# Three seams of an eight-sublayer network on one core: a stage's last group finished inside the next stage, ends beside batches, norms on ScalarE

## The chip, the cores and the metric

The kernel is one program on one core of a Trainium2 chip. It holds five engines with a queue each: TensorE (PE, with its weight loads listed as PEld), VectorE (DVE), ScalarE (ACT), GpSimd (POOL) and SyncE (SP), which issues all the DMAs of this kernel. Each engine works through its own queue in order. The metric is the device time of one execution in microseconds. The time before is the median of three runs.

## The reference

The network has four layers, each of an attention-like and a feed-forward sublayer, over 16 sequences of 256 tokens with 128 features:

```python
x = L0_attn_inputs                                   # (16, 256, 128), float32
x = x + _layernorm(_L0_attn_ref(_layernorm(x), ...)) # attention with masked scores
x = x + _layernorm(_L0_ffn_ref(_layernorm(x), ...))  # gated, weights from int32
x = x + _layernorm(_L1_attn_ref(_layernorm(x), ...)) # 4 blocks: mixed attention + MLP
x = x + _layernorm(_L1_ffn_ref(_layernorm(x), ...))  # soft mixture of 64 experts
x = x + _layernorm(_L2_attn_ref(_layernorm(x), ...)) # 16-head causal attention
x = x + _layernorm(_L2_ffn_ref(_layernorm(x), ...))
x = x + _layernorm(_L3_attn_ref(_layernorm(x), ...)) # scan, MLP, attention, MLP
x = x + _layernorm(_L3_ffn_ref(_layernorm(x), ...))  # experts chosen by top-k

def _layernorm(x, axis=-1, eps=1e-05):
    m = jnp.mean(x, axis=axis, keepdims=True)
    v = jnp.var(x, axis=axis, keepdims=True)
    return (x - m) / jnp.sqrt(v + eps)
```

Within `_L1_attn_ref` each of the four depths first normalises x again with a gain and a bias (`ln1_g`, `ln1_b`) and adds its attention, then does the same with `ln2_g`, `ln2_b` and an MLP with gelu. The mixture of `_L1_ffn_ref` is the part with two softmaxes:

```python
logits = jnp.einsum('bmd,dnp->bmnp', x, phi)
dispatch = jax.nn.softmax(logits, axis=0)            # over the 16 sequences
combine = jax.nn.softmax(logits.reshape(bsz, m, n * p), axis=-1).reshape(bsz, m, n, p)
slots = jnp.einsum('bmd,bmnp->bnpd', x, dispatch)
y = jnp.einsum('bnpd,nde->bnpe', slots, W) + b[None, :, None, :]
out = jnp.einsum('bnpd,bmnp->bmd', y, combine)
```

## The kernel before

The tokens lie in SBUF as eight groups, x[0] to x[7]. A group is two sequences: 128 partitions by NT = 4 tiles of 128 tokens by D = 128 features. z[0] to z[7] hold the input of a sublayer in the same form. The program is a row of stages: stage_l0 (layer 0, both sublayers), stage_l1_attn, stage_soft_moe (the mixture), stage_l2_attn and so on. Each stage opens a pool of work tiles in SBUF and one in PSUM, and closes them when it has emitted its last instruction. The next stage's tiles lie in the same memory, so its first instructions on those tiles wait until the last instructions of the closed pools have ended. The names of PSUM tiles in the profile are those of the rings (ps_s, ps_o, ps_mm, ps_t), whichever computation uses them.

A layer norm is made of these pieces. `stats` (L243 to L257 in the profile) gives four BATCH_NORM_STATS2 (ln_st) and four aggregates (ln_mv) on VectorE, then `rsqrt` on GpSimd: a TENSOR_SCALAR (L244) and a power (L245), both of 128x4, which give rs. `normed` (L264) subtracts the mean and multiplies by rs in four TENSOR_SCALAR on VectorE. In stage_l0 there is another form of its own, which makes nb = -mean * rs on GpSimd (L577, L578) and then normalises with four ACTIVATE on ScalarE (L583). `residual` normalises y into ln_y and adds it to x on GpSimd (L284).

The pieces of work of one group are Python generators. What follows a `yield` is emitted later, after what the other active generators emit. stage_l0 gives its order by hand (`turns`, a group every four steps). stage_l1_attn uses `interleave` with five active generators: the 8 `l1_mix` and then the 8 `ffn` generators of each of the four depths. `l1_norm_T` at the head of each makes a norm, four transposes against the identity (L306) and a copy with gain and bias on ScalarE (L776), and gives hT (xT in the profile) to the projections wq, wk and tok. In `l1_mix` VectorE reduces the first part of tok (qm, q; L831, L832) and the maxima of the scores (l_max, L854), then adds them into q2T (L868); the second scores give e (ScalarE, L901), masked on GpSimd (L904), and oT (L917). In the last depth `ffn` goes on with the residual to x[g] and with `then(g)`, which is `fill`: it stores x[g] to DRAM as xs and makes mxn[g], the norm that the mixture reads. Outside the stages ordered by hand a scheduler places the instructions of the generators on the engines' queues; the final order on each queue is fixed when the program is built.

stage_l1_attn begins with its constants: six memsets of l1_val and l1_lin, four of l1_max and l1_ctx, two copies into l1_ctx, all on GpSimd (L746 to L750), and two casts on VectorE (L753).

The mixture works through eight blocks of experts. In turn n it runs `share(n)`, `logits(n + 2)` and `slots(n + 1)` side by side. `share` takes the 16 sequences b in turn: exponentials, four transposes, a copy (meT), the product with y (ps_o), and two updates of x per b on VectorE (L1145), with the sums copied by ScalarE (mgot, L1148). In the last turn, when only `share` is left, the two sequences of a group are followed by `end(g)`:

```python
back = k.t([P, NT, D], "slT", 3)
nc.sync.dma_start(out=back, in_=xs[:, g])
...
v.tensor_tensor(xg, xg, bc(r.rearrange("p t b -> p b t"), 3, D), ALU.mult)
n = yield from k.norm(x[g], "mdisp", 3)
nc.gpsimd.tensor_tensor(x[g], back, n, ALU.add)
```

Here r (mend in the profile, L1164 to L1166) is one over the sum of weights, L1168 is the multiplication, mdisp the normalised result and L1170 the addition on GpSimd. stage_l2_attn then begins with `head(0)`, whose norm (xn) comes from x[0], and with `attention_pools`, memsets of at_vm and at_pc on GpSimd (L344 to L349) and casts on VectorE (L356). The keys are spread over heads as km (two ACTIVATE, one GpSimd product L364), and only then does the first score matmul run.

Of the kernel before, what the change touches and what calls it, by code (L numbers as in the profile page):

```python
# [185 lines left out]
def idle(n):  # L186

    for _ in range(n):
        yield


def bc(ap, axis, n):

    ap = ap.unsqueeze(axis)
    shape = list(ap.shape)
    shape[axis] = n
    return ap.to_broadcast(shape)


class Ctx:  # L200
# [61 lines left out]
    def normed(self, out, src, mv, rs):  # L262
        for k in range(NT):
            self.nc.vector.tensor_scalar(  # L264
                out[:, k, :], src[:, k, :], mv[:, k, 0:1], rs[:, k : k + 1], ALU.subtract, ALU.mult
            )
# [277 lines left out]
def stage_l0(k, x, w, wv, wi, z):  # L544
# [27 lines left out]

    def stats(src):

        mv, rs = k.stats(src)
        nb = k.t([P, NT], "ln_nb", 6)
        gp.tensor_scalar(nb, mv[:, :, 0], -1.0, None, ALU.mult)  # L577
        gp.tensor_tensor(nb, nb, rs, ALU.mult)  # L578
        return nb, rs

    def normed(out, src, nb, rs):
        for t in range(NT):
            nc.scalar.activation(  # L583
                out[:, t, :], src[:, t, :], AF.Identity, bias=nb[:, t : t + 1], scale=rs[:, t : t + 1]
            )
# [62 lines left out]
    def group(g):  # L648
        nb, rs = stats(x[g])
        yield from idle(2)  # L650
        xn = k.t([P, NT, D], "xn", 2)
        normed(xn, x[g], nb, rs)
# [38 lines left out]
        nb, rs = stats(x[g])  # L691
        yield from idle(2)
        xn = k.t([P, NT, D], "xf", 2)
        normed(xn, x[g], nb, rs)
# [23 lines left out]
        y = k.t([P, NT, D], "y", 3)  # L718
        nc.scalar.copy(y, ps)
        yield  # L720
        mv, rs = k.stats(y)
# [4 lines left out]
        nb, rs = stats(x[g])  # L726
        yield from idle(2)
        normed(z[g], x[g], nb, rs)
        yield

# [4 lines left out]
def stage_l1_attn(k, x, ws, rows, z, then):  # L735
# [9 lines left out]
    for a in k.l1_val + k.l1_lin:  # L745
        nc.gpsimd.memset(a, 1.0)  # L746
# [17 lines left out]
    for i in range(4):  # L764
        steps += [l1_mix(k, z[g], ws[i], rows[f"bo{i}"], NG * i + g) for g in range(NG)]
        steps += [ffn(i, g) for g in range(NG)]
        leads += [4] * NG + [2] * NG
    k.interleave(steps, 5, leads, -1)
# [28 lines left out]
def l1_mix(k, z, w, bo, n):  # L797
# [7 lines left out]
    hT = yield from l1_norm_T(k, z, w["ln1_g"], w["ln1_b"])  # L805
# [146 lines left out]
def soft_inputs(k, x, pool):  # L952

    xs = k.dram.tile([P, NG, NT, D], F32, tag="xs", name="xs")
    xn = [pool.tile([P, NT, D], F32, tag=f"mxn{g}", name=f"mxn{g}") for g in range(NG)]

    def fill(g):
        k.nc.sync.dma_start(out=xs[:, g], in_=x[g])
        yield from k.norm_to(xn[g], x[g])

    return xs, xn, fill


def stage_soft_moe(k, x, w, wdram, bdram, xn, xs):
# [9 lines left out]
    xT = {}  # L974
# [147 lines left out]
    def share(n):  # L1122
# [3 lines left out]
        for b in range(NB):  # L1126
# [21 lines left out]
            nc.scalar.copy(got[:, :, b], ps[:, :, D])  # L1148
            yield
            if n == blocks - 1 and b % 2:  # L1150
                yield from end(b // 2, f, got)
# [6 lines left out]
    def end(g, f, got):  # L1158

        back = k.t([P, NT, D], "slT", 3)  # L1160
        nc.sync.dma_start(out=back, in_=xs[:, g])
        bs = slice(2 * g, 2 * g + 2)
        r = k.t([P, 2, 2], "mend", 2)
        v.tensor_tensor(r, sums[:, :, bs], f[:, :, bs], ALU.mult)  # L1164
        v.tensor_tensor(r, r, got[:, :, bs], ALU.add)
        v.reciprocal(r, r)  # L1166
        xg = x[g].rearrange("p (b t) d -> p b t d", b=2)
        v.tensor_tensor(xg, xg, bc(r.rearrange("p t b -> p b t"), 3, D), ALU.mult)  # L1168
        n = yield from k.norm(x[g], "mdisp", 3)
        nc.gpsimd.tensor_tensor(x[g], back, n, ALU.add)  # L1170

    for n in range(-2, blocks):
# [6 lines left out]
        while parts:  # L1179
            parts = [p for p in parts if next(p, k) is not k]  # L1180


def stage_l2_attn(k, x, w, beside):
# [3 lines left out]
    def head(g, got):  # L1187
        yield
        xn = yield from k.norm(x[g], "xn", 1, 2)
        yield  # L1190
# [591 lines left out]
def program(ctx: ExitStack, tc: tile.TileContext, xin, dram, at, out):  # L1782
# [46 lines left out]
    nc.gpsimd.memset(k.mhalf, -0.5)  # L1829
    rows1 = load_rows(base, "l1rows")  # L1830
# [17 lines left out]
    stage("l0", "left", stage_l0, l0, l0v, l0f, z, banks=ONE_RING)  # L1848
# [5 lines left out]
    stage("l1a", "left", stage_l1_attn, l1, rows1, z, fill, banks=RING_BANKS)  # L1854
# [56 lines left out]
```

## Time and profile before

| what | value |
|---|---|
| median of three runs | 3017.48 us (3016.08 to 3022.56) |
| time of the profiled execution | 3016.38 us |
| its span | 3014.7 us |
| granted TensorE clock, mean | 0.962 |
| busy: TensorE, VectorE, ScalarE, GpSimd | 2753.9, 1999.3, 1607.1, 1010.7 us |
| first matmul of block 1 | 187.45 us |
| last mxn of block 1's attention starts | 963.20 us |
| last addition of the mixture starts | 1553.99 us |
| first matmul of layer 2's attention | 1562.11 us |

The page gives the span in 40 slices, a busy share for each engine, and groups of instructions named by line, engine, tile written and tile read, with count, total and mean. The timeline lists instructions in order of time: start, length, engine, line, operation, tiles, and in square brackets the idle time of that engine before them and what ended it. Table rows by stretch give, for a piece of the span, the busy time of PE, PEld, DVE, ACT and POOL with the number of instructions, then the granted clock, the DMA share and GB/s. Times in the text without another word are microseconds from the start of the span.

### The profile page before, as it was taken

The numbers are of one execution on the slowest core, as the hardware profiler recorded it, in microseconds if no ns is written. First come the engines' busy times: TensorE is split into PE (matmuls) and PEld (weight loads), VectorE is DVE, ScalarE is ACT, GpSimd is POOL, SyncE is SP. The second block draws the span as 40 slices with busy tenths as digits, with TensorE's granted clock in tenths as the row PEclk, the third lists the DMA queues.
The fourth block names the chain that finished last, engine by engine and source line by source line (L and its number), as shares of the span: only waits on it lengthen the run. The fifth ranks groups of instructions, "written<-read, shape, count | busy, mean of one in ns | idle before, by whom it ended". The sixth has DMA issues, their size and how long they took to land.

```text
span 3014.7 us, 59480 instructions
## 1 busy us (share of the span) xinstructions
PE 2753.9 (91%) x23674; PEld 1882.7 (62%) x23674; DVE 1999.3 (66%) x5462; ACT 1607.1 (53%) x3376; POOL 1010.7 (34%) x1368
## 2 busy tenths in 40 slices
PE   8979999999997799999959997899999699978898
PEld 4647766777666588888743443566666344436897
DVE  5667465574657989999776774565765577638542
ACT  6745556555563567767615665344443377642332
POOL 3553333333335100000044554322222466553332
PEclk9989999999998899999979998899999799988999
DMA  4000000000000000000110000000000000010000
GB/s 114 11 1 2 1 2 2 1 2 1 2 5 33 1 16 8 8 8 8 31 50 1 1 1 1 1 1 1 1 1 2 1 1 1 1 57 1 1 15 15
DMA packets 29150, 31.30 MB, mean 10 GB/s; under 512 B 7292, under 2 KB 20156, under 8 KB 28732
## 3 DMA queue, kind: packets, MB, share of 16 engines
q1 hardware_dynamic: 28872, 27.49, 3.1%
q8 instruction: 187, 3.06, 0.4%
q14 instruction: 91, 0.75, 0.1%
HBM read 23.29 MB, written 4.19 MB: 9 GB/s over the span
## 4 chain that ended last, share of the span: by engine, by line
PE 48%; DVE 9%; ACT 6%; POOL 3%; issue 2%; DMA 0%; POOLq 0%; SPq 0%; ACTq 0%; DVEq 0%
PE ps_s L317 30%; PE ps_o L317 7%; PE ps_mm L317 6%; ACT at_e L472 1%; ACT lg L1129 1%; PE ps_s L306 1%; POOL ln_rs L245 1%; ACT meT L1136 1%; PE ps_sum L317 1%; ACT mdisp L1036 1%; DVE ln_st L255 1%; ACT lg L1009 1%; PE ps_s L506 1%; PE ps_t L1134 1%; DVE at_nm L440 1%
## 5 line engine op out<-in xcount | busy, mean ns | idle before, releaser
L244 POOL TENSOR_SCALAR ln_rs<-ln_mv 128x4 f32<-128x4 f32 x192 | 40.2, 209 | 849.5 <-DVE ln_mv L257 827.8
L440 DVE TENSOR_REDUCE at_nm<-ps_s 128x2 f32<-128x512 f32 (+1 forms) x384 | 238.0, 681 | 122.3 <-PE ps_s L317 122.3
L472 ACT ACTIVATE at_e<-ps_s 128x512 f32<-128x512 f32 x384 | 198.1, 604 | 92.5 <-PE ps_s L317 90.3
L1391 DVE TENSOR_TENSOR scan<-ps_s,lm 128x384 f32<-128x384 f32 x256 | 124.6, 548 | 143.3 <-PE ps_s L317 143.0
L478 POOL TENSOR_SCALAR_AFFINE_SELECT at_e<-at_e 128x1024 f32<-128x1024 f32 (+1 forms) x96 | 135.1, 1408 | 215.5 <-ACT at_e L472 215.2
L245 POOL TENSOR_TENSOR ln_rs<-ln_rs,mhalf 128x4 f32<-128x4 f32 x192 | 196.0, 1021 | 15.7
L854 DVE TENSOR_REDUCE l_max<-ps_s 128x3 f32<-128x384 f32 x256 | 124.0, 547 | 64.1 <-PE ps_s L317 64.1
L317 PE MATMUL ps_o<-my,meT 128*128 128x129 f32 x1024 | 144.4, 288 | 18.8 <-ACT mgot L1148 16.1
L317 PEld LDWEIGHTS ps_s<-l_w,mlp_h 128*128 128x128 f32 x1280 | 149.4, 192 | 19.0 <-issue 15.3
L317 PE MATMUL ps_s<-l1f_phi,mxT 128*128 128x256 f32 x512 | 141.5, 399 | 16.8 <-DVE mpart L1010 16.8
L317 PEld LDWEIGHTS ps_o<-my,meT 128*128 128x128 f32 x1024 | 128.0, 195 | 37.0 <-ACT mgot L1148 22.5
L317 PE MATMUL ps_s<-km,qT 32*128 32x512 f32 x768 | 139.8, 659 | 11.9 <-POOL km L364 10.5
L317 PE MATMUL ps_s<-l_w,mlp_h 128*128 128x128 f32 x1280 | 150.2, 275 | 0.3
L317 PE MATMUL ps_s<-qm,kT 32*128 32x512 f32 x768 | 143.8, 655 | 5.2 <-DVE at_nm L440 5.0
L904 POOL TENSOR_SCALAR_AFFINE_SELECT e<-e 128x512 f32<-128x512 f32 x128 | 78.5, 634 | 178.5 <-ACT e L901 178.5
L317 PE MATMUL ps_o<-at_e,at_vm 128*32 128x128 f32 (+1 forms) x2048 | 122.7, 336 | 15.2 <-ACT at_oT L502 15.2
L317 PE MATMUL ps_mm<-mdisp,mxn 128*128 128x128 f32 x1024 | 125.3, 279 | 5.0 <-DVE mdisp L1048 4.9
L901 ACT ACTIVATE e<-ps_s 128x384 f32<-128x384 f32 x256 | 105.6, 513 | 39.7 <-PE ps_s L317 39.6
L317 PEld LDWEIGHTS ps_mm<-mdisp,mxn 128*128 128x128 f32 x1024 | 121.8, 195 | 7.9 <-DVE mdisp L1048 6.6
L317 PE MATMUL ps_s<-xT,l_w 128*128 128x512 f32 x256 | 119.3, 596 | 2.7 <-ACT mlp_h L789 2.7
L1368 ACT COPY BT<-ps_s 128x512 f32<-128x512 f32 x64 | 37.5, 586 | 154.6 <-PE ps_s L317 154.6
L317 PEld LDWEIGHTS <-b_ident 128*128 128x128 bf16 x656 | 51.4, 98 | 109.3 <-issue 99.5
(427 smaller groups left out, 7098.4 us busy)
## 6 DMA issues: line engine op xcount, KB each, us to landing
mw<-in_l1fw SPq DMA_DIRECT2D x16, 256.0 KB, 2.7
moe_w<-in_moe SPq DMA_DIRECT2D x16, 256.0 KB, 5.3
l_w<-in_l SPq DMA_DIRECT2D x10, 256.0 KB, 3.3
x<-in_x SPq DMA_DIRECT2D x8, 256.0 KB, 4.3
xs<-x SPq DMA_DIRECT2D x8, 256.0 KB, 2.0
slT<-xs SPq DMA_DIRECT2D x8, 256.0 KB, 2.8
out<-x SPq DMA_DIRECT2D x8, 256.0 KB, 2.3
l1f_phi<-in_l1f SPq DMA_DIRECT2D x1, 1024.0 KB, 4.9
```

Source lines behind the costliest of these rows:

```text
L244: g.tensor_scalar(out, in_, scale, eps, ALU.mult, ALU.add)
L245: g.tensor_tensor(out, out, self.mhalf[:, :n], ALU.pow)
L255: v.bn_stats(out=st[:, k, :], in_=src[:, k, :])
L317: self.nc.tensor.matmul(out, lhsT=lhsT, rhs=rhs, start=start, stop=stop, skip_group_check=True)
L440: v_.tensor_reduce(nm[:, t, r, vs], s, AX.X, ALU.max, negate=True)
L472: nc.scalar.activation(e[:, r], s, AF.Exp)
L478: nc.gpsimd.affine_select(at, at, [[0, 4], [0, n], [1, P]], ALU.is_ge, 0.0, base=0, channel_multiplier=-1)
L854: v.tensor_reduce(mx[:, b, :, h, 16], s, AX.X, ALU.max, negate=True)
L901: nc.scalar.activation(e[:, h].rearrange("p j n -> p (j n)"), s[:, : 3 * P], AF.Exp)
L904: nc.gpsimd.affine_select(e[:, :, j, :], e[:, :, j, :], [[0, 4], [1, P]], ALU.is_ge, 0.0, base=0, channel_multiplier=-1)
L1368: nc.scalar.copy(s, ps)
L1391: v.tensor_tensor(m, s[:, : SEQ + P], lm[:, SCAN_HEADS[4 * (t // 2) + 2 * i + hh], :], ALU.mult)
```

## The change

It has four parts.

1. Group 7 of stage_l0 stops after its y, which is kept in a tile of its own (hand_y). The residual and the norm that gives z[7] run as `rest_of_l0` inside stage_l1_attn, one step of it for each step of the first `l1_mix`.
2. Group 0 of stage_l0 goes on: it also makes the first norm of stage_l1_attn and its transpose, with gain and bias, in a tile hand_xT. The first `l1_mix` takes it in place of its own. The six memsets of l1_val and l1_lin go to VectorE.
3. `fill` normalises mxn on ScalarE, with nb from GpSimd.
4. In the mixture `end` is appended to the list of generators that run side by side, instead of being run to its end by `share`. It no longer multiplies x by r. It takes mean and variance of the unscaled x, forms rt, one over the sum of weights, and gets the scale as rt * (var * rt * rt + eps)^-0.5, with three more products of 128x4 on GpSimd. After group 0's end, its statistics for the next stage are made and kept in two tiles that outlive the stage; head(0) of stage_l2_attn only normalises with them, on ScalarE.

```diff
+    def stats_nb(self, src, kept=None):
+        mv, rs = self.stats(src)
+        g = self.nc.gpsimd
+        nb, to = kept or (self.t([P, NT], "ln_nb", 6), rs)
+        g.tensor_scalar(nb, mv[:, :, 0], -1.0, None, ALU.mult)
+        g.tensor_tensor(nb, nb, rs, ALU.mult)
+        if kept:
+            g.tensor_copy(to, rs)
+        return nb, to
+
+    def normed_act(self, out, src, nb, rs):
+        for t in range(NT):
+            self.nc.scalar.activation(
+                out[:, t, :], src[:, t, :], AF.Identity, bias=nb[:, t : t + 1], scale=rs[:, t : t + 1]
+            )
...
-        y = k.t([P, NT, D], "y", 3)
+        y = y7 if g == NG - 1 else k.t([P, NT, D], "y", 3)
         nc.scalar.copy(y, ps)
         yield
+        if g == NG - 1:
+            return
...
+        if g == 0:
+            nb, rs = k.stats_nb(z[g])
+            yield from idle(2)
+            xn = k.t([P, NT, D], "xf", 2)
+            k.normed_act(xn, z[g], nb, rs)
+            yield
+            ps = k.transposed_ps(xn)
+            nc.scalar.activation(xT0, ps, AF.Identity, bias=l1["ln1_b"], scale=l1["ln1_g"])
+            yield
...
+def rest_of_l0(k, x, z, y):
+    yield from k.residual(x, y)
+    yield
+    nb, rs = k.stats_nb(x)
+    yield
+    k.normed_act(z, x, nb, rs)
...
     for a in k.l1_val + k.l1_lin:
-        nc.gpsimd.memset(a, 1.0)
+        nc.vector.memset(a, 1.0)
...
+    def beside(a, b):
+        for _ in a:
+            next(b, k)
+            yield
+
+    steps[0] = beside(steps[0], rest_of_l0(k, x[NG - 1], z[NG - 1], y7))
...
-    hT = yield from l1_norm_T(k, z, w["ln1_g"], w["ln1_b"])
+    if hT is None:
+        hT = yield from l1_norm_T(k, z, w["ln1_g"], w["ln1_b"])
...
         k.nc.sync.dma_start(out=xs[:, g], in_=x[g])
-        yield from k.norm_to(xn[g], x[g])
+        nb, rs = k.stats_nb(x[g])
+        yield
+        k.normed_act(xn[g], x[g], nb, rs)
...
-            yield
             if n == blocks - 1 and b % 2:
-                yield from end(b // 2, f, got)
+                parts.append(end(b // 2, f, got))
+            yield
...
-        v.reciprocal(r, r)
-        xg = x[g].rearrange("p (b t) d -> p b t d", b=2)
-        v.tensor_tensor(xg, xg, bc(r.rearrange("p t b -> p b t"), 3, D), ALU.mult)
-        n = yield from k.norm(x[g], "mdisp", 3)
-        nc.gpsimd.tensor_tensor(x[g], back, n, ALU.add)
+        rt = k.t([P, NT], "mendt", 3)
+        v.reciprocal(rt.rearrange("p (b t) -> p t b", b=2), r)
+        st = k.t([P, NT, 6], "ln_st", 3)
+        mv = k.t([P, NT, 2], "ln_mv", 6)
+        for t in range(NT):
+            v.bn_stats(out=st[:, t, :], in_=x[g][:, t, :])
+        for t in range(NT):
+            v.bn_aggr(out=mv[:, t, :], in_=st[:, t, :])
+        rs = k.t([P, NT], "ln_rs", 6)
+        gp.tensor_tensor(rs, mv[:, :, 1], rt, ALU.mult)
+        gp.tensor_tensor(rs, rs, rt, ALU.mult)
+        k.rsqrt(rs, rs, 1.0, LN_EPS)
+        gp.tensor_tensor(rs, rs, rt, ALU.mult)
+        yield
+        n = k.t([P, NT, D], "mdisp", 3)
+        k.normed(n, x[g], mv, rs)
+        gp.tensor_tensor(x[g], back, n, ALU.add)
+        yield
+        if g == 0:
+            k.stats_nb(x[g], k.kept)
...
+        if g == 0:
+            xn = k.t([P, NT, D], "xn", 1)
+            k.normed_act(xn, x[g], *k.kept)
+            yield from idle(3)
+        else:
+            xn = yield from k.norm(x[g], "xn", 1, 2)
+            yield
```

## The prediction

> **What bounds the kernel now.** I read the page first, then the busy times by stretch, then the waits and the timeline at three places where TensorE stands still.
>
> ```profile
> span 3014.7 us, 59480 instructions
> PE 2753.9 (91%) x23674; PEld 1882.7 (62%) x23674; DVE 1999.3 (66%) x5462; ACT 1607.1 (53%) x3376; POOL 1010.7 (34%) x1368
> ...
> 170.00:187.40 17.40, 0.00 (x0) 0.00 (x0) 8.23 (x51) 3.76 (x9) 11.74 (x27) 0.65 0.00 1
> 187.40:230.00 42.60, 40.64 (x360) 27.24 (x364) 32.23 (x120) 21.03 (x57) 20.00 (x28) 0.90 0.01 2
> 899.00:948.30 49.30, 48.53 (x302) 37.15 (x300) 39.13 (x169) 20.66 (x30) 28.41 (x38) 1.00 0.09 33
> 948.30:965.10 16.80, 1.97 (x8) 1.56 (x8) 13.99 (x63) 0.56 (x1) 8.99 (x15) 0.65 0.08 32
> 1505.00:1540.00 35.00, 26.17 (x172) 22.62 (x170) 27.56 (x119) 10.56 (x29) 12.38 (x15) 0.86 0.40 123
> 1540.00:1562.10 22.10, 0.94 (x7) 0.77 (x6) 15.79 (x56) 0.33 (x2) 13.89 (x23) 0.58 0.03 7
> ```
>
> Each row is: stretch, length, busy us of PE, weight load, VectorE, ScalarE, GpSimd, granted clock, DMA share, GB/s. TensorE is busy 91% of the span, so time comes back only where it is idle. The change touches the three rows with PE near zero: 17.4 + 14.8 + 21.2 = 53 us, 1.8% of the span. None of it can exceed that. DMA moves almost nothing there.
>
> ```profile
> 169.88 0.58 ACT L719 COPY y<-ps_s 128x512 f32<-128x512 f32 x1 [3.32 <-PE ps_s L317]
> 178.69 1.65 ACT L583 ACTIVATE z<-x,ln_nb,ln_rs 128x128 f32<-128x128 f32 x4 [5.95 <-POOL ln_nb L578]
> 180.45 1.59 POOL L746 MEMSET l_val<- 128x512 f32 x3 [1.79 <-issue]
> 187.45 1.15 PE L306 MATMUL ps_s<-const_ident,xn 128*128 128x128 f32 x4 [17.61 <-DVE xn L264]
> ...
> 954.03 0.68 DVE L794 TENSOR_TENSOR z<-ps_s,z 128x512 f32<-128x512 f32 x1
> 963.20 1.11 DVE L264 TENSOR_SCALAR mxn<-x,ln_mv,ln_rs 128x128 f32<-128x128 f32 x4 [1.42 <-POOL ln_rs L245]
> ...
> 1519.19 1.11 DVE L1165 TENSOR_TENSOR mend<-mend,mgot 128x4 f32<-128x4 f32 x1
> 1535.71 1.12 DVE L264 TENSOR_SCALAR mdisp<-x,ln_mv,ln_rs 128x128 f32<-128x128 f32 x4 [1.11 <-POOL ln_rs L245]
> 1537.39 1.33 DVE L1168 TENSOR_TENSOR x<-x,mend 128x512 f32<-128x512 f32 x1
> 1555.31 1.80 POOL L344 MEMSET at_vm<- 128x2048 f32 x1
> 1562.11 1.08 PE L306 MATMUL ps_s<-const_ident,xn 128*128 128x128 f32 x4 [21.17 <-DVE xn L264]
> ```
>
> At each place the pattern is one: the last group's norms run as a serial chain VectorE, GpSimd, VectorE; only when its last instruction ends does the next stage touch its memory (180.4, 964.4, 1555.3); then GpSimd memsets and another norm follow before the first transpose.
>
> **Part 1, seam from block 0 to block 1 (170 to 230).** Group 7's y now goes to hand_y and its two norms leave stage_l0. The release moves from 180.34 (end of z for group 7) to the end of z for group 6, 171.10 + 1.65 = 172.75: 7.6 us. Group 0's norm and transpose are ready (hand_xT), so TensorE can start wq after the hand_y copy, 170.5 instead of 189.5. But the queues decide what follows. VectorE after the release, in its new order: six memsets (no such row on VectorE; GpSimd's took 0.53 and 0.27 each, so 2.4; bounds 1.0 to 3.3), two casts 0.6 to 1.2, statistics of hand_y 1.2, then the first qm/q 1.2: q ends near 178. It then waits for hand_y's rs (GpSimd 1.3 after 176.8), ln_y 1.1, the first four maxima 1.9 (end 181), statistics of x 1.2, four maxima 1.9, statistics of group 1 1.2, q2T 0.7. Group 1's xn, needed by a transpose that stands before the first q2T matmul in TensorE's queue, ends near 188.7. First e near 190 against 208.13 before: 18 us ahead. This lead is partly paid back: before, xn of three groups (5.08) and their statistics were made in the dead time; now they lie between. From 188.7 VectorE does xn for groups 2 and 3, each behind 1.3 of GpSimd and a 1.27 addition, and reaches group 1's qm at 197.5. ScalarE's second half of e stands behind that (200.2), its mask and products end near 205, against oT at 214.85: 9.8 ahead, with 2.2 of score work not yet done. The second maxima of group 1 end near 208.4 against 215.0: 6.6 ahead. The periods are then 15.93 (oT at 214.85, 230.8), bound by TensorE. I take 7 (from 5.8, the VectorE path with slow memsets, to 12, if TensorE catches up during the ramp). Group 7's residual (3.5 VectorE, 1.65 ScalarE, 4.3 GpSimd) is in this sum.
>
> Price in block 0: group 0's extra norm is 1.2 VectorE, 1.75 GpSimd, 0.6 TensorE, 1.65 + 0.78 ScalarE. ScalarE is nearly full there (from 85.5 to 104.6 it idled 3.75 in 19.1), so I charge 1.5 (0.6 to 2.4). Net -5.5.
>
> A clock rule: the two wq matmuls took 2.08 at 189.5 and 1.02 later, with the clock at 0.65 and 0.90 in the rows above. The Trainium skill ("TensorE: Matmul & The Clock Gate", Part 1) says an idle window of about 3.4 us halves the clock. With 0.6 us idle the new start is warm; the new ramp has holes of about 4 us (176.5 to 181) that could make it cold again, about 1.7 each by the rule. TensorE is not the bound in the ramp, so I count 0; by the rule it would be up to +3.4.
>
> **Part 2, end of block 1's attention (900 to 965).** The four mxn VectorE instructions per group go to ScalarE. Eight groups cost 15.5 us (mean 543 ns, one of four caught behind GpSimd's addition, 1.29). TensorE is dense to 948.2, so not all of the 15.5 can be gained, only VectorE's lag behind TensorE. Group 7's addition to z came at 954.03, 5.8 after its last matmul. Without mxn a late period of VectorE is 6.6 - 2.0 = 4.6, below TensorE's 7.45, so the lag vanishes. Chain from 948.3: z 0.7, statistics 1.2, rs 1.4, ln_y 1.1 (952.8); GpSimd first finishes group 6's nb (953.35), addition 1.3, statistics 1.2, rs and nb 1.9, four ACTIVATE 1.65: 959.6 against 964.3. Added GpSimd: 16 x 0.22. Net -4.7 (-6.5 to -1).
>
> **Part 3, mixture's ends (1506 to 1562).** Before, one group took 5.75 of VectorE: mdisp 1.03, small ones and three x updates 0.9, the multiplication L1168 1.25, statistics 1.15, then 1.43 until rs. The multiplication goes. GpSimd's chain grows by two products in front and one behind: 0.08 + 0.31 + 0.31 + 0.28 + 1.02 + 0.04 + 0.2 + 0.05 = 2.3. In VectorE's new order mdisp still stands behind only two x updates (0.6) after the statistics, so it waits this out: 1.03 + 0.55 + 1.5 + 2.3 = 5.4 a group. "Beside" is thus true of the order, not of the time. Group 0's kept statistics also stand ahead of group 1's chain: + 1.9 once; group 0 is 0.5 earlier. Then the added question: the new mend pair runs 0.6 after mdisp, during GpSimd's addition (1.27). Row 1519.19 shows such a mend taking 1.11 instead of 0.15. The Trainium skill ("SBUF — State Buffer", Who interferes with whom) states the lock for it: two SBUF inputs on VectorE against a GpSimd instruction that reads SBUF. By the rule 0.75 more each, 6.3 a group, and the last addition ends near 1559.8 instead of 1555.25 (+4.5); by the plain row of 0.15, 1554.4 (-0.9). I take +2.5, nearer to the rule, because the trace has its case.
>
> The head of the next stage then needs no statistics. Before: release 1555.29 to the first km matmul 1568.71, 13.4. Now: four ACTIVATE 1.65, transposes and copy to +2.9, kT copied at +5.7, GpSimd's memsets end at +6.6 as before, km 1.9: first km matmul at +8.5. Net -4.9. Together -2.4 (-6 to 0). SP: the fourth reload of xs stands three issues earlier and l_o and two more weights wait behind it for group 0's addition; these serve a stage that starts hundreds of us later, so nothing. If the reload itself were late (2.8 to landing), the addition would wait, but the buffer is free two groups ahead.
>
> **Sum.** -5.5 - 4.7 - 2.4 = -12.6: span 3014.7 to 3002.1. The profiled execution took 3016.38 (1.7 around the span) and the median is 1.1 above it: 3004.9, given as 3004.
>
> **The rivals.** *All seams convert:* memsets short, no lock on mend, TensorE refills the ramp: -12 + 0.6, -6.5, -0.9 - 4.9: -23.7, about 2993. For it: the 53 us of idle PE. Against: VectorE's order above.
>
> *The change does not do what it says:* ends cost +4.5, memsets and the cold clock take part 1 to -2.5, ScalarE's new waits part 2 to -2: about -5, 3012. For it: row 1519.19 and the 2.3 us chain.
>
> *Slower, through ScalarE's queue at the end of block 1:* in the new order the fourth gelu of each of five groups stands behind the first mxn, which waits for nb. In the old timeline rs was ready at 918.36, nb would be near 918.8, and the gelu it would hold ran at 915.89: 3.4 late. With a 1.27 addition in front on GpSimd, about 5. If TensorE, dense there, loses all of it: 5 x 5 = 25, total -12.6 + 25 = +12.4, 3030. It decides from 3.7 each (5 x 3.7 = 12.6 + 6). Against: that gelu belongs to the first half of the next group, whose second product runs a period (7.45) later, and ScalarE is busy only 20.7 of 49.3.
>
> **How the numbers follow.** A measurement of this kernel can tell 0.2%, 6 us, from no change. Forecast 0.55, all seams 0.22, does not do what it says 0.17, slower 0.06. Faster: 0.55 x 0.95 + 0.22 + 0.17 x 0.3 = 0.79; same 0.15; slower 0.06. The forecast's own bounds are 2994 to 3012; the range reaches to the rivals on both sides, 2990 to 3014.
>
> **What would show it.** Right: first block 1 matmul near 170.5 but oT of group 0 near 207, the maxima with waits before them; the last mxn ending near 954 (959.6 less 5.5); mdisp in the mixture waiting about 1.6 for GpSimd and a period near 5.4 to 6.3; no statistics before the first transpose of the next attention and 8.5 from release to km. Wrong: a gain of first oT above 12, a period below 5, holes in TensorE between 900 and 948, or a shift elsewhere.

## The result and the profile after

The changed kernel takes 3005.63 us (median of five runs, 3001.13 to 3007.66) against 3018.27 (3016.08 to 3022.56) for the kernel before on the same chip: ratio 0.9953, 95% interval 0.9939 to 0.9966, or 12.6 us less (10 to 18 by the interval). The forecast was 3004, 12.6 less by its own sum. The profiled execution became 9.8 us shorter (3014.7 to 3004.9). The sum came out; several of its terms did not, and that is what the experiments are about.

The first two lines of the page after:

```profile
span 3004.9 us, 59512 instructions
...
PE 2762.2 (92%) x23674; PEld 1886.5 (63%) x23674; DVE 1977.8 (66%) x5420; ACT 1623.0 (54%) x3416; POOL 1020.3 (34%) x1407
```

TensorE has the same 23674 products, yet they took 8.3 us longer (2753.9 before). The products are the same, so the clock is the first suspect: by the profile's records of the clock TensorE was busy 142.5 us at half clock, against 129.7 before, which is an estimated 6.4 of the 8.3. The busy times by stretch, at the three seams (columns as before: PE, weight load, VectorE, ScalarE, GpSimd, granted clock, DMA share, GB/s):

```profile
173.40:174.10 0.70, 0.03 (x2) 0.02 (x1) 0.00 (x0) 0.59 (x1) 0.70 (x1) 1.00 0.00 0
174.10:216.00 41.90, 35.47 (x256) 22.44 (x256) 32.55 (x146) 18.58 (x47) 23.99 (x40) 0.80 0.01 2
894.00:944.00 50.00, 48.42 (x301) 36.77 (x299) 32.60 (x169) 27.97 (x52) 33.87 (x54) 1.00 0.09 32
944.00:955.40 11.40, 1.09 (x9) 0.86 (x9) 5.37 (x31) 4.75 (x12) 6.64 (x15) 0.63 0.12 46
1499.00:1535.00 36.00, 24.21 (x169) 20.23 (x166) 24.49 (x119) 10.53 (x28) 17.38 (x37) 0.94 0.39 118
1535.00:1551.50 16.50, 2.12 (x9) 1.83 (x9) 9.34 (x41) 1.07 (x5) 9.52 (x18) 0.50 0.02 9
```

The stretches of 17.4, 16.8 and 22.1 us in which TensorE did little are now 0.7, 11.4 and 16.5 long. Behind the first of them new holes have opened: TensorE idles 6.4 us in the 41.9 of the next row (2.0 in 42.6 before). That row has a granted clock of 0.80 where the kernel before had 0.90.

The timeline at the first seam, on ScalarE, VectorE and TensorE (a group's start, its time, and in brackets the idle time before it with what ended it):

```profile
173.44 0.59 ACT L725 COPY hand_y<-ps_s 128x512 f32<-128x512 f32 x1 [3.32 <-PE ps_s L336]
174.67 1.65 ACT L283 ACTIVATE z<-x,ln_nb,ln_rs 128x128 f32<-128x128 f32 x4 [0.65 <-POOL ln_nb L275]
176.55 1.57 DVE L772 MEMSET l_val<- 128x512 f32 x3 [3.79 <-ACT z L283]
174.08 1.13 PE L336 MATMUL ps_s<-hand_xT,l_wq 128*128 128x512 f32 x2 [0.68 <-ACT hand_y L725]
183.29 2.11 PE L336 MATMUL ps_s<-kT,qT 32*128 32x128 f32 x12 [2.43 <-DVE l_max L889]
195.10 2.08 PE L336 MATMUL ps_s<-xT,l_wq 128*128 128x512 f32 x2
```

TensorE idles 0.68 until hand_y's copy has ended and starts wq of group 0 at full clock (1.13 for two). The first block 1 product was forecast near 170.5 and stands at 174.08. Inside the hole of 2.43 that ends at 183.29 the clock halves, at 182.29 by its record and until 199.35, and the wq of group 1 at 195.10 takes 2.08. hand_y's copy stands at 173.44, where y of group 7 stood at 169.88: block 0 became 3.56 longer. oT of group 0 comes at 207.65 (before 214.85).

The end of block 1's attention, and then the end of the mixture with the head after it:

```profile
943.65 0.69 DVE L827 TENSOR_TENSOR z<-ps_s,z 128x512 f32<-128x512 f32 x1 [1.17 <-PE ps_s L336]
953.08 1.65 ACT L283 ACTIVATE mxn<-x,ln_nb,ln_rs 128x128 f32<-128x128 f32 x4 [2.62 <-POOL ln_nb L275]
...
1524.97 1.12 DVE L264 TENSOR_SCALAR mdisp<-x,ln_mv,ln_rs 128x128 f32<-128x128 f32 x4 [1.77 <-POOL ln_rs L1217]
1526.51 0.93 DVE L1203 TENSOR_TENSOR mend<-sums,mfade 128x4 f32<-128x4 f32 x1
1530.90 1.11 DVE L264 TENSOR_SCALAR mdisp<-x,ln_mv,ln_rs 128x128 f32<-128x128 f32 x4 [1.77 <-POOL ln_rs L1217]
...
1549.62 1.26 POOL L1221 TENSOR_TENSOR x<-slT,mdisp 128x512 f32<-128x512 f32 x1 [1.23 <-DVE mdisp L264]
1551.47 1.63 PE L325 MATMUL ps_s<-const_ident,xn 128*128 128x128 f32 x4 [14.06 <-ACT xn L283]
1558.58 1.14 PE L336 MATMUL ps_s<-km,qT 32*128 32x512 f32 x8
```

The addition to z of group 7 waits for TensorE again instead of lagging it. The ends have a period of 5.93 (5.75 before); mdisp waits 1.77 for GpSimd's ln_rs, and mend's small product takes 0.93 instead of 0.15. Each span's own times, set against each other, split the 9.8 us so:

| stretch | before | after | change |
|---|---|---|---|
| start to the addition to z that began at 887 before (part 1) | 887.15 | 881.80 | -5.35 |
| from there to the mixture's first instruction, the cast of mquarter (part 2) | 77.25 | 73.01 | -4.24 |
| mixture, to the first x update of the last turn (nothing changed there) | 541.55 | 545.16 | +3.61 |
| first x update to last addition (part 3, ends) | 49.30 | 50.91 | +1.61 |
| last addition to first km product (part 3, head) | 13.46 | 7.70 | -5.76 |
| from there to the end | 1445.99 | 1446.32 | +0.33 |

The times of the addition to z are its starts; the expectations below call them ends. Two things were not in the forecast as they came: block 0 became 3.56 us longer inside the first row (1.5 was charged), and the mixture 3.6, where no instruction was changed.

### The profile page after: what moved, and what is told of

It is laid out like the page before. It is cut to its first block, busy times and chain, and to the rows that moved or that the text cites. A ratio compares the mean times of both kernels' runs of the same rounds, so it can differ in the third digit from the quotient of the medians.

```text
span 3004.9 us, 59512 instructions
## 1 busy us (share of the span) xinstructions
PE 2762.2 (92%) x23674; PEld 1886.5 (63%) x23674; DVE 1977.8 (66%) x5420; ACT 1623.0 (54%) x3416; POOL 1020.3 (34%) x1407
## 4 chain that ended last, share of the span: by engine, by line
PE 73%; DVE 10%; ACT 9%; POOL 5%; issue 3%; DMA 0%; POOLq 0%; ACTq 0%; DVEq 0%
PE ps_s L336 51%; PE ps_o L336 8%; PE ps_mm L336 6%; PE ps_s L325 2%; POOL ln_rs L245 2%; ACT at_e L491 1%; DVE ln_st L255 1%; ACT lg L1166 1%; ACT meT L1173 1%; PE ps_sum L336 1%; ACT mdisp L1073 1%; ACT lg L1046 1%; PE ps_s L973 1%; ACT e L936 1%; DVE ln_y L264 1%
## 5 line engine op out<-in xcount | busy, mean ns | idle before, releaser
L336 PEld LDWEIGHTS ps_s<-l_w,mlp_h 128*128 128x128 f32 x1280 | 149.4, 192 | 19.0 <-issue 15.3
L336 PEld LDWEIGHTS ps_o<-my,meT 128*128 128x128 f32 x1024 | 127.9, 195 | 41.9 <-ACT mgot L1185 25.5
L336 PE MATMUL ps_o<-at_e,at_vm 128*32 128x128 f32 (+1 forms) x2048 | 122.7, 336 | 15.3 <-ACT at_oT L521 15.3
```

What stands on the lines that cost most here:

```text
L336: self.nc.tensor.matmul(out, lhsT=lhsT, rhs=rhs, start=start, stop=stop, skip_group_check=True)
```

## The experiments

The times of one kernel spread by some 6 us between executions, and by 12 in one case below, so small edits are read from stretches of the trace; the times are given beside them. "Changed" is the changed kernel. All times are medians; ratios are against the kernel before, run beside it.

**The changed kernel once more, for a second trace.** No edit.

> The changed kernel once more, for a second trace. In the first one the mixture lasted 545.2 us from its first transpose (954.76) to the first x update of its last turn (1499.97); in the kernel before 541.4 (964.54 to 1505.95), with the same instructions in the same order. The 3.8 lie in three short stretches of a halved TensorE clock: 60 products of mdisp and mxn took 8.59 us instead of 6.96. Theory (the clock's windows fall where they fall, not the program): in a second execution the stretches lie elsewhere, and the mixture lasts between 541 and 545, not 545.2 again; hand_y's copy stays near 173.4, since the hole that opens there is the program's. Rival (the change itself makes these windows cold): 545.2 within 0.3 again, with the same 60 products at 8.6. Time 3005.6 by both, within 3.

Measured: 3004.01 us, ratio 0.9954 (0.994 to 0.9969); mixture 542.7, hand_y's copy at 174.04. One line of the timeline, TensorE's 60 products of mdisp and mxn, from the kernel before, the changed one, and this second execution of it, and under them the stretch around them in the first two. The third block holds slices of 3.41 us, the steps in which the profile records the clock: two of the changed kernel's first trace, and two of its second:

```profile
1020.88 6.96 PE L317 MATMUL ps_mm<-mdisp,mxn 128*128 128x128 f32 x60 [1.06 <-DVE mdisp L1048]
...
1011.30 8.59 PE L336 MATMUL ps_mm<-mdisp,mxn 128*128 128x128 f32 x60 [1.06 <-DVE mdisp L1085]
...
1014.49 6.96 PE L336 MATMUL ps_mm<-mdisp,mxn 128*128 128x128 f32 x60 [1.06 <-DVE mdisp L1085]
```

```profile
1018.00:1035.00 17.00, 14.58 (x151) 12.75 (x151) 16.42 (x20) 8.81 (x15) 0.00 (x0) 1.00 0.00 1
...
1008.40:1025.40 17.00, 15.34 (x147) 13.61 (x146) 15.48 (x19) 7.20 (x14) 0.00 (x0) 0.90 0.00 1
```

```profile
1008.32:1011.73 3.41, 1.75 (x8) 1.11 (x8) 3.41 (x4) 2.22 (x5) 0.00 (x0) 1.00 0.00 0
1011.73:1015.14 3.41, 3.41 (x18) 3.41 (x17) 3.31 (x7) 0.59 (x1) 0.00 (x0) 0.50 0.00 0
...
1009.38:1012.79 3.41, 2.44 (x10) 1.52 (x9) 2.93 (x5) 3.41 (x9) 0.00 (x0) 1.00 0.00 0
1012.79:1016.20 3.41, 2.35 (x18) 1.92 (x18) 3.41 (x5) 0.94 (x2) 0.00 (x0) 1.00 0.00 0
```

The same instructions behind the same hole of 1.06 us took 1.63 longer in one execution and not in the other. In the first this hole and one of 0.60 before it lie in one slice, which leaves TensorE 1.75 us busy, and the next slice is granted 0.50. In the second the edge of a slice falls between the two holes, each slice keeps more than 2.3 us busy, and the clock stays. (In the kernel before, the slice with the hole of 1.06 had 1.84 us busy, and the clock stayed too.) In the changed kernel's first trace this happened at three places of the mixture (losses of 1.6, 1.0 and 1.0, read from the mdisp instructions of the two traces). Over the fourteen traces of this study the mixture lasted from 541.5 to 545.2; the kernel before was at the short end and the changed one at the long end by accident. So the 3.6 are not the change's. The Trainium skill ("TensorE: Matmul & The Clock Gate", Part 1) says that the window over which TensorE's activity is judged runs free of the kernel; the two executions above agree, as the same products meet the slices at another place. It shows in the times too: in one of the kernels below, 3006.5 us came with a mean clock of 0.964 and 3018.3 with 0.958.

**Group 0's extra norm later in block 0.**

```
         if g == 0:
+            yield from idle(10)
             nb, rs = k.stats_nb(z[g])
```

> The changed kernel, with group 0's extra norm in block 0 started ten turns later (its ScalarE instructions then stand near 150 instead of 105). Theory: block 0 became 3.56 us longer (copy to hand_y at 173.44 instead of 169.88) because the four ACTIVATE stood ahead of group 3's and 4's work on a full ScalarE (+1.8), which opened a hole of 2.65 on TensorE, and a halved clock after it (+1.6: 24 products of f_down took 3.56 instead of 2.94, two of l_wk 1.92 instead of 1.02). Late in the block ScalarE has room: hand_y's copy near 170.3, oT of group 0 near 204.6 instead of 207.7, total -3: 3002.6. Rival (the norm costs its work wherever it stands, through TensorE's order and the ring of banks): copy near 173, total 3005.6.

Measured: 3001.39 us, ratio 0.9945 (0.9931 to 0.996); end of hand_y's copy at 171.04 instead of 174.03, oT at 205.39. Where the 3.56 came from shows at the next group, from the changed kernel, its second execution, and this one (the hole before TensorE's transposes of e, and the 24 products of f_down after it):

```profile
115.73 0.93 PE L636 MATMUL ps_s<-const_ident,e 128*128 128x128 f32 x4 [2.65 <-ACT e L628]
119.55 3.56 PE L336 MATMUL ps_s<-f_down,h 128*128 128x128 f32 x24
...
119.60 0.93 PE L636 MATMUL ps_s<-const_ident,e 128*128 128x128 f32 x4 [2.64 <-ACT e L628]
122.39 2.94 PE L336 MATMUL ps_s<-f_down,h 128*128 128x128 f32 x24
...
115.58 0.93 PE L636 MATMUL ps_s<-const_ident,e 128*128 128x128 f32 x4 [1.31 <-ACT e L628]
118.38 2.95 PE L336 MATMUL ps_s<-f_down,h 128*128 128x128 f32 x24
```

From the y copy of group 3 to that of group 4 it took 19.1 us in the kernel before and in this one, 20.8 in the changed kernel's second execution, and 22.5 in its first. So the norm's four ACTIVATE on a full ScalarE cost 1.7; the hole that they open (2.65 instead of 1.31) cost another 1.6 in the execution where the clock halved behind it. Of the eight traces with the norm at this place, five paid 1.7 and three 3.4 to 4.3. Moved to where ScalarE has room, the norm costs block 0 nothing. The gain in the median is within the spread, and so the time alone does not decide against the rival; the intervals do. (Intervals are compared here, since the first 31 us of block 0 already differ by up to 4 between executions of the same instructions: the third xn starts at 27.27 in the first trace of the changed kernel and at 31.15 in the second. The cause of that I did not look for.)

**mdisp two turns later in the ends.**

```
         gp.tensor_tensor(rs, rs, rt, ALU.mult)
-        yield
+        yield from idle(3)
         n = k.t([P, NT, D], "mdisp", 3)
```

> The changed kernel, with each end's mdisp on VectorE two turns later, so that the next batches' x updates and the next group's statistics stand ahead of it. Theory: of the period of 5.94 VectorE worked 4.17 and waited 1.77 for GpSimd's ln_rs; with the wait filled the period is 4.3 to 4.7, seven periods give 9, the last group's own chain stays: total -8.5, 2997. Rival (the batches hold the period: one bank for ps_o, product 1.16, x update 0.57, mgot 0.16, meT 0.59 and a transpose in a ring, about 2.8 each): period 5.5 to 5.9, total -0 to -3, 3003 to 3005.6.

Measured: 2990.87 us, ratio 0.9912 (0.9895 to 0.9929), clear of the changed kernel's interval; first x update to last addition 35.6 instead of 50.9. One period of the ends, in the changed kernel and two here, and mdisp with mend here:

```profile
1524.97:1530.90 5.93, 2.98 (x20) 2.35 (x20) 4.16 (x19) 1.49 (x5) 3.08 (x6) 1.00 0.15 44
...
1517.88:1521.23 3.35, 2.09 (x16) 1.66 (x15) 3.35 (x21) 1.30 (x4) 3.02 (x7) 1.00 0.27 81
1521.23:1524.57 3.34, 1.48 (x13) 1.29 (x11) 3.34 (x21) 0.32 (x2) 3.01 (x7) 1.00 0.25 83
```

```profile
1517.88 1.14 DVE L264 TENSOR_SCALAR mdisp<-x,ln_mv,ln_rs 128x128 f32<-128x128 f32 x4
1519.47 0.15 DVE L1203 TENSOR_TENSOR mend<-sums,mfade 128x4 f32<-128x4 f32 x1
```

VectorE is full (3.35 of 3.35), GpSimd nearly (3.02). These are two of the steady periods; the one that holds group 0's kept statistics still takes 7.4, and an edit that moves these was not tried. The wait of 1.77 is gone, and with it 0.8 of VectorE's own "work": mend takes 0.15 again, as it no longer falls into GpSimd's addition. My expected 4.3 to 4.7 had counted that blocked time as work. The rival falls: the batches' ring did not hold the period; it was itself held by the x updates that stood behind the waiting mdisp.

**mdisp on ScalarE.** rs and mean make a bias nb on GpSimd (two more small products), and four ACTIVATE take mdisp's place one turn later.

```
-        yield
+        nb = k.t([P, NT], "ln_nb", 6)
+        gp.tensor_scalar(nb, mv[:, :, 0], -1.0, None, ALU.mult)
+        gp.tensor_tensor(nb, nb, rs, ALU.mult)
+        yield from idle(2)
         n = k.t([P, NT, D], "mdisp", 3)
-        k.normed(n, x[g], mv, rs)
+        k.normed_act(n, x[g], nb, rs)
```

> The changed kernel, with each end's mdisp made by ScalarE (four ACTIVATE of 0.41 with -mean*rs as bias, two more small GpSimd products) one turn later. Theory: VectorE has 3.1 a group left and waits for GpSimd no more; ScalarE has about 2 + 1.65; the period falls to the batches' own ring, 4.5 to 5, total -6 (the last group's chain is 0.5 + 0.6 longer): 2999.6. Rival (the wait only changes engines: the ACTIVATEs wait for nb at the head of ScalarE's queue and hold mgot and meT of the next batch, so TensorE's next product): period 5.9 or more, total 0 to +3: 3005.6 to 3008.6.

Measured: 3002.19 us, ratio 0.9945 (0.993 to 0.996); the ends in 47.75, period 5.7. ScalarE's timeline:

```profile
1526.69 1.26 ACT L283 ACTIVATE mdisp<-x,ln_nb,ln_rs 128x128 f32<-128x128 f32 x3 [2.96 <-POOL ln_nb L1220]
1527.86 0.14 ACT L1185 COPY mgot<-ps_o 128x2 f32<-128x2 f32 x1
```

The wait moved to ScalarE (2.96), and mgot, which frees the bank of ps_o for TensorE, stands behind it. The period lies between the two expectations, nearer to the rival's: taking the norm off VectorE and leaving a wait saved 3.2 of the ends, filling the wait 15.3.

**Part 2 undone: mxn on VectorE.**

```
-        nb, rs = k.stats_nb(x[g])
-        yield
-        k.normed_act(xn[g], x[g], nb, rs)
+        yield from k.norm_to(xn[g], x[g])
```

> The changed kernel, with part 2 alone undone: mxn on VectorE again (four instructions of about 0.54 a group, right after the statistics). Measured from the addition to z that ended at 882 to the cast of mquarter, the first instruction of the mixture, the kernel before took 77.25 us and the changed one 72.9 to 73.0 in five traces. Theory (VectorE's 15.5 us of mxn made it lag TensorE by 5.8 at the end, and that is all part 2 gains): this stretch returns to 77.2, and the time rises by 4.3, 3009.5 (within 3 for the clock's windows elsewhere). Rival (the lag went through the order of the queues, or ScalarE's new waits took part of the gain, so that VectorE does it as well): the stretch stays at 73 to 75, time 3005 to 3007.

Measured: the stretch took 77.3 us, against 77.25 before and 72.9 to 73.0 in every kernel with part 2; 3006.83 us, ratio 0.9963 (0.9948 to 0.9977). The theory's number. The part of it from that addition to z to the one of group 7 took 66.9 before and here, and 61.9 in the changed kernel, which is the lag that goes. The time itself cannot tell 4 us here.

**Part 1 undone.** stage_l0 ends group 7 itself, hand_y and hand_xT stay unused, and the memsets are GpSimd's.

```
-        if g == NG - 1:
-            return
...
-    steps[0] = beside(steps[0], rest_of_l0(k, x[NG - 1], z[NG - 1], y7))
...
-        nc.vector.memset(a, 1.0)
+        nc.gpsimd.memset(a, 1.0)
```

> The changed kernel, with part 1 alone undone: group 7 ends inside block 0, no norm is made ahead, the memsets are GpSimd's. Theory (part 1 is worth 5.3, of which 3.56 was paid in block 0): y of group 7 is copied at 170 instead of 173.4 to 174.6, oT of group 0 near 214.8, the addition to z that ends at 882 to 884 in the changed kernel ends at 887; from there on as in the changed kernel (73.0 to the mixture, 50.9 for its end); time +5.3, 3010 (within 3). Rival (TensorE is the bound of block 1's attention, and what the ramp gains is given back there): z at 882 to 884 all the same, time 3005.

Measured: 3011.11 us, ratio 0.9977 (0.9964 to 0.999). From the end of y's copy to the addition to z it takes 716.5 (716.7 before), and 707.5 to 709.9 with all of part 1: a gain of 6.8 to 9.2 that is not given back later. That addition began at 889.4 instead of 887, as this execution reached the y copy 2.4 later than the kernel before did. Counted from group 3's y copy, which ends just ahead of the extra norm, to the addition to z, the price in block 0 is in the sum: 786.1 and 784.3 in the two traces without part 1, 779.3 to 781.5 (mean 780.1) in the seven with all of it at its first place, a net gain of 5.2 in the mean.

**The ends as before, the head kept.** The old end() in line with the batches, and behind it `if g == 0: k.stats_nb(x[g], k.kept)`.

> The changed kernel, with the ends of the mixture as in the kernel before (x multiplied by mend, statistics, mdisp, in line with the batches), group 0's statistics for the next stage still made ahead. From the first x update of the last turn to the last addition the kernel before took 49.3, the changed one 50.9, the one with mdisp two turns later 35.6. Theory (putting the ends beside the batches gained nothing, since mdisp waits 1.77 for GpSimd on VectorE as before, and the gain of this seam is all the head's): 49.3 + 1.2 for group 0's statistics = 50.5, the head as in the changed kernel (0.6 to the first transpose), total -0.4: 3005 (within 3). Rival (taking 8 multiplications of 1.25 off VectorE is what paid for the longer chain): 57 to 60, total +6 to +9, 3012 to 3015.

Measured: 51.2 from the first x update to the last addition (changed: 50.9); 3004.38 us, ratio 0.9956 (0.9942 to 0.9971). The theory's number: the new ends as a whole, beside the batches, without the multiplication and with the longer chain on GpSimd, gained 0.3. The next experiment, in which the statistics are gone from the new ends, puts it at 1.0 (48.3 against 49.3).

**The head as before.**

```
-        if g == 0:
-            xn = k.t([P, NT, D], "xn", 1)
-            k.normed_act(xn, x[g], *k.kept)
-            yield from idle(3)
-        else:
-            xn = yield from k.norm(x[g], "xn", 1, 2)
-            yield
+        xn = yield from k.norm(x[g], "xn", 1, 2)
+        yield
...
-        yield
-        if g == 0:
-            k.stats_nb(x[g], k.kept)
```

> The changed kernel, with the head of the next attention as in the kernel before: group 0's statistics are made there, not kept from the mixture. Theory (this norm is all that the seam of part 3 gains): the last turn loses group 0's statistics, which stretched one period from 5.94 to 7.78, so its x updates to the last addition take 49.1 instead of 50.9; from the last addition to the first km product 13.4 as before instead of 7.7; together +3.9, 3009 (within 3 for the clock). Rival (GpSimd's memsets of at_vm, not the statistics, hold the first km product): 8 to 10 all the same, total -1 to +1: 3005.

Measured: 3008.45 us, ratio 0.9967 (0.9957 to 0.9977). The last addition ended at 1547.06, and TensorE's timeline is:

```profile
1553.04 1.08 PE L325 MATMUL ps_s<-const_ident,xn 128*128 128x128 f32 x4 [19.45 <-issue]
1560.34 1.14 PE L336 MATMUL ps_s<-km,qT 32*128 32x512 f32 x8
```

13.3 to the first km product (7.7 with the kept norm): the norm with its statistics, not GpSimd's memsets, held it. The ends took 48.3, so keeping group 0's statistics there costs 2.6, and the head is worth 3.0 net.

**Part 1 without the norm made ahead.** Group 7 is still handed on.

```
-        steps += [l1_mix(k, z[g], ws[i], rows[f"bo{i}"], NG * i + g, xT0 if i + g == 0 else None) for g in range(NG)]
+        steps += [l1_mix(k, z[g], ws[i], rows[f"bo{i}"], NG * i + g) for g in range(NG)]
```

> The changed kernel without group 0's norm made ahead in block 0: group 7's y is still handed on and block 1 still starts after group 6's z, but norms group 0 itself. From hand_y's copy to the oT of group 0 the kernel before took 44.4, the changed one 33.6 (35.3 in three other traces). Theory (the early release is the larger half; the norm made ahead is worth the chain of statistics 1.2, GpSimd 1.3, xn 1.1, transposes 1.2, copy 0.8, less what stands behind VectorE's memsets anyway, 3 to 4): 37 to 39, hand_y's copy 1.7 earlier at least, since the extra norm no longer stands on ScalarE; total +1 to +2, 3006.5 (within 3). Rival (the norm made ahead is what brings the gain, since VectorE's queue sets the ramp and this puts group 0's norm back in front of it): 42 to 44, total +5 or more, 3010.

Measured: 3008.47 us, ratio 0.9972 (0.9958 to 0.9986); 41.1 from the end of hand_y's copy (173.02) to group 0's oT: of the 10.8 gained, the early release brings 3.3 and the norm made ahead 7.5 (5.8 against the traces of the changed kernel that took 35.3). The rival was nearer (42 to 44); my theory's 37 to 39 failed. The timelines of TensorE and VectorE show where the time lies:

```profile
181.12 1.15 PE L325 MATMUL ps_s<-const_ident,xn 128*128 128x128 f32 x4 [8.73 <-DVE xn L264]
183.19 2.08 PE L336 MATMUL ps_s<-xT,l_wq 128*128 128x512 f32 x2 [0.92 <-ACT xT L800]
...
189.84 1.11 DVE L264 TENSOR_SCALAR xn<-z,ln_mv,ln_rs 128x128 f32<-128x128 f32 x4 [1.86 <-POOL ln_rs L245]
190.87 0.28 DVE L857 TENSOR_REDUCE qm<-ps_s 128x8 f32<-128x128 f32 x1
```

The first qm comes 17.9 after hand_y's copy, instead of 6.1 (180.13). Most of these 11.8 us are the later start of TensorE: its transposes wait for group 0's norm, wq starts 10.2 after hand_y's copy instead of at its end, and at half clock (2.08 for two instead of 1.13). On VectorE qm then stands behind the xn of a second group, 2.2 after its product is done, about as long as it stood behind the memsets and statistics before (2.3).

**The memsets on GpSimd.** `nc.vector.memset(a, 1.0)` is `nc.gpsimd.memset(a, 1.0)` again.

> The changed kernel with the six memsets of l_val and l_lin on GpSimd again, as in the kernel before; they took 2.4 on VectorE. Theory (VectorE's queue sets the ramp, the prediction's path began with these memsets): hand_y's copy to the oT of group 0 shrinks from 33.6 to 31.5 or so, total -1 to -2, 3004 (within 3). Rival (GpSimd's queue takes over: its 2.4 of memsets and the four others stand ahead of the chain for hand_y's rs, for which the first maxima wait, and VectorE's casts wait for them): 33.6 to 36, total 0 to +2.

Measured: hand_y to oT 34.3 (33.6 to 35.3 in the other traces), 3005.95 us, ratio 0.996 (0.9945 to 0.9975). That lies where the rival put it, but also within the spread of the traces without this edit: which engine makes the memsets made no difference that could be told.

**Both edits.** The extra norm and mdisp later.

> The changed kernel with two edits at once: mdisp two turns later (alone: 2990.9, the ends in 35.6 instead of 50.9) and group 0's extra norm ten turns later in block 0 (alone: 3001.4, hand_y copied at 171.0 instead of 173.4 to 176). Theory (two places that have nothing to do with each other): the gains add, hand_y at 171, ends 35.6, total 2990.9 - 3.0 = 2988. Rival (the 3 us of block 0 are given back to halved clocks further on, as in the mixture): hand_y at 171, but the stretch from there to the mixture's first instruction is 3 longer, total 2991.

Measured: 2991.07 us, ratio 0.9911 (0.9896 to 0.9926); end of hand_y's copy at 171.36, ends 35.9, span 2985.3. The stretch from hand_y to the mixture is no longer than elsewhere, so the rival's reason is not seen; but the median is that of the ends' edit alone. Whether the 2 to 3 us of block 0 add to it can't be told at this spread.

**Norms of the ramp on ScalarE.** Both edits, and for groups 1 to 3 of the first layer l1_norm_T uses `k.stats_nb` and `k.normed_act`.

> The kernel of the two edits (mdisp two turns later, extra norm later; 2991.1), and in addition block 1's norms of groups 1 to 3 in the first layer on ScalarE (four ACTIVATE 1.65 with nb) instead of VectorE (four of 1.1 to 1.8 each). From hand_y's copy to the oT of group 0 it took 33.6. In that ramp VectorE waited 3.3 us for ln_rs ahead of these three norms (0.27 + 1.34 + 1.72) and worked 4.2 on them. Theory (VectorE's waits for GpSimd, in the order of its queue, set the ramp as they set the mixture's ends): 33.6 falls to 29 to 31, total -3, 2988 (within 3). Rival (TensorE and ScalarE's own order set it; the ACTIVATEs wait for nb at the head of ScalarE's queue and hold xT, qT and the halves of e): 33 to 36, total 0 to +2, 2991 to 2993.

Measured: 2989.42 us, ratio 0.9901 (0.9884 to 0.9917), not to be told from 2991; hand_y to oT 34.3. VectorE idled 6.3 in one piece (195 to 201.6) and the ramp was no shorter. The ramp by stretch, in this kernel:

```profile
184.00:188.00 4.00, 4.00 (x28) 2.49 (x25) 4.00 (x18) 0.70 (x2) 1.61 (x4) 0.50 0.00 0
188.00:192.00 4.00, 1.22 (x4) 0.71 (x4) 4.00 (x29) 2.68 (x8) 2.07 (x5) 0.50 0.00 0
192.00:196.00 4.00, 4.00 (x17) 1.98 (x18) 3.28 (x25) 1.27 (x3) 3.23 (x7) 0.50 0.00 0
196.00:200.00 4.00, 4.00 (x10) 1.78 (x7) 0.00 (x0) 3.06 (x8) 3.67 (x8) 0.50 0.00 0
```

TensorE is busy 4.00 of 4.00 in three of the four rows, at half clock. From 195 on VectorE waits for TensorE (its idle 6.3 ended with a product in ps_s), so here TensorE, at half clock, sets the end of the ramp. The other traces fit: of the eleven with the norm made ahead, the three whose clock halved once more for 6.8 us near 204 took 35.3 to 35.4 from hand_y to oT, the eight others 33.6 to 34.4.

## Why the prediction was right, and where it was not

**Part 1, -5.5 against -5.35.** The net is right, and not by this one pair alone: 5.2 in the mean of the traces. The terms are less so, and two errors cancel: block 0 took more than was charged, the ramp behind it less, so that oT came at 207.65, near the 207 that was named, from a start 3.6 too late. The price in block 0 was put at 1.5 (0.6 to 2.4); ScalarE's share of it measured 1.7, but the profiled execution paid 3.56, since the hole that the delay opened halved the clock behind it, which the step did not weigh at all. The gross gain was put at 7 and measured 8.9 in this pair, 6.8 to 9.2 over the traces. Its way there failed: I walked VectorE's queue and started with 2.4 of memsets, but moving these or taking norms off VectorE (34.3 each, against 33.6 to 35.4) shortened nothing. And the step "TensorE is not the bound in the ramp, so I count 0" is wrong for its end: TensorE ran at half clock from 182 to 199, busy nearly throughout but for two holes. The forecast had +3.4 for this from the Trainium skill ("TensorE: Matmul & The Clock Gate", Part 1), and set it aside; 14.0 us of busy time at half clock in those 17.1 are, as an estimate, up to 7 us of slowed products. How much of it stands on the path, and what keeping TensorE warm there would bring, was not tried. That page puts the halving after an idle window of about 3.4 us; here less idle time was enough: in the slice of 3.41 us ahead of the halving in the ramp TensorE was still busy 1.66, in that of block 0 1.62.

**Part 2, -4.7 against -4.24.** Right, and for its reason: VectorE's lag of 5.8 went (group 7's addition to z waits 1.17 for TensorE), GpSimd's nb and the four ACTIVATE came. With mxn back on VectorE the stretch returned to 77.3. The slower rival, a gelu held behind mxn, did not come: between 894 and 944 TensorE was busy 48.42 of 50 at a clock of 1.00.

**Part 3, ends +1.61 against +2.5.** The mechanism is the predicted one: mdisp waits 1.77 for GpSimd (predicted about 1.6), mend is blocked by the addition (0.93 instead of 0.15), group 0's kept statistics stretch one period to 7.78, and the period of 5.93 lies between the plain 5.4 and the blocked 6.3 (which by its own 0.75 for the lock should read 6.15). The size was off by 0.9. The ends put back changed 50.9 into 51.2: beside was true of the order only. One reason why dropping eight multiplications of 1.25 gained so little stands in the kernel before: most of them ran into GpSimd's addition. The row at 1537.39 has 1.33; this one, at 1520.80, came after the addition had ended:

```profile
1520.80 0.68 DVE L1168 TENSOR_TENSOR x<-x,mend 128x512 f32<-128x512 f32 x1
```

So about 0.65 of each was waiting beside GpSimd, and in the new order mend's product waits there instead (0.78).

**Part 3, head -5.76 against -4.9.** 7.7 to the first km product instead of 8.5; the 13.3 of the undone head shows the cause. Keeping the statistics costs 2.6 in the ends, so this part is worth 3.0 net.

**Not in the sum.** The mixture's +3.6 is where three stretches of halved clock fell in that one execution. A shift elsewhere was named as a sign of being wrong; it came, and the second execution (542.7) shows that it is not the change's. It explains why the profiled pair gives 9.8 where the medians give 12.6. The forecast took one profiled execution as exact to 1 us; the fourteen traces say 2 to 4. That sum and median agree to 0.1 us is therefore luck; that they agree within a few us is not. The bound of 53 us was also too low: it left out the 8.8 us that TensorE idles in the row 1505 to 1540, which the ends touch too.

## What to carry to other kernels

When a step is put "beside" other work, look at what stands behind its waiting instruction on an in-order queue: here one instruction that waited 1.77 us for GpSimd held the x updates, and through them ScalarE and TensorE, and issuing it two turns later was worth as much again as the whole change (15.3 us in the ends; 13 to 15 between the medians, against 12.6). A short delay on a nearly full engine costs its own length and possibly a stretch of halved TensorE clock after the hole that it opens; place extra work where that engine has room (1.7 us of ScalarE in block 0 became 3.4 to 4.3 in three traces of eight, and 0 once moved). Compare edits of a few us by stretches of several traces, not by one span: identical instructions differed by 3.6 us between executions.

## What the hardware showed that was not expected

Holes of 0.60 and 1.06 us in one slice of 3.41 us, which left TensorE 1.75 busy, were followed by 60 products at 8.59 us; in another execution of the same kernel the slices lay otherwise, and they took 6.96. Over the fourteen traces (without their first 10 and last 20 us) all 251 full-clock slices in which TensorE was busy less than 1.45 us were followed by a halved one, 64 of the 188 with 1.45 to 2.0, and 23 of the 10852 busier ones. It is the busy time within such a slice, not the length of one hole, that goes with the halving. Blocked time is booked as busy time: VectorE's 4.16 of each period contained 0.8 of mend waiting beside GpSimd's addition, so that the engine looked nearer to its limit than it was; the steady period went down to 3.35.
